# Issuing the stores of the stages between the loops from SyncE instead of ScalarE: a selective-scan and attention kernel on Trainium2

## The chip, the cores and the metric

The kernel runs on one core of a Trainium2 chip. The metric is the device time of one execution in microseconds (us). Engines are named as in the profile: PE (TensorE), DVE (VectorE), ACT (ScalarE), POOL (GpSimd) and SP (SyncE). A transfer between memories (DMA) is started by an instruction in the queue of one engine, here ACT or SP; the profile writes ACTq and SPq for such instructions. Each engine works through its own list of instructions, and they meet through semaphores.

## The reference

Four images of 64 x 64 tokens with 96 channels go through four layers. Layers 0 and 1 are the ones that the change touches: group norm, an input projection to 192 channels with a gate z, a depthwise 3 x 3 convolution, a selective scan in four directions (rows, columns, and both backwards), layer norm, the gate, an output projection and a residual sum. Layers 2 and 3 are linear attention and a feed-forward network on the tokens. The part behind the transfers in question, cut to what matters:

```python
x_dbl = jnp.einsum('bkdl,kcd->bkcl', xs, x_proj_weight)
dts, Bmat, Cmat = jnp.split(x_dbl, [R, R + N], axis=2)
delta = jax.nn.softplus(jnp.einsum('bkrl,kdr->bkdl', dts, dt_projs_weight) + dt_projs_bias[None, :, :, None])
...
def step(h, inp):
    u, d, b, c = inp
    dA = jnp.exp(d[..., None] * A)
    h = dA * h + d[..., None] * b[:, :, None, :] * u[..., None]
    y = jnp.einsum('bken,bkn->bke', h, c)
    return (h, y)
```

For each direction the kernel therefore needs three things before the scan: delta, the product delta times u (called du), and the rows B and C (called bc).

## The kernel before, in words

**Phases.** A pair of images in one of the two scan layers is a phase; there are four. `run` (L701) goes through them: for phase p it runs `prepare` (L151), in which `finish` (L548) of phase p - 1 is mixed by means of Python generators, and then `scan_phase` (L471), the loop. After the fourth loop the last `finish` runs alone, and `token_layers` follows. What the change calls the stages between the loops are `prepare` and `finish`; intermediate results go from them to the loops, and back, through buffers in HBM (`ph.delta`, `ph.du`, `ph.bc`, `ph.ud`, `ph.y`).

**prepare.** It reads the input, makes the group norm statistics, and calls `convolve` (L234) for the first image of the pair. `convolve` loads raw slices (rawi, L244, by SP), normalises them into a padded image xn (L248, DVE), runs nine matmuls for each chunk of 512 positions (L263), and writes Silu of the sum to xc (L270, ACT). It ends with sixteen pieces of xu, xc scaled by the skip weights (L277, ACT), each stored to `ph.ud` (L283). Then for each of the two images, eight chunks and two directions with their backward twins, `steps` (L285) runs: 32 calls, each one step in what follows. The second image's `convolve` is mixed into the first image's steps. The generator's yields and `ph.beside` set how many pieces of the previous phase's `finish` are placed beside each step: 0.5 during the second convolution, 1.7 after it.

**A step.** PE projects the chunk (L292); ACT copies the result to xd in both time directions (L295, L296), and bc is stored from it (L304, two stores, one for each direction). PE makes delta's argument (L309), and then for each of the two directions: ACT softplus to dl (L317) and a bf16 copy to parts[0] (L318); DVE du = dl times u (L319) and the remainder dl - parts[0] (L320); two stores of du to two copies in HBM (L322); POOL parts[1] (L323), DVE parts[2] (L324): delta is kept as three bf16 terms; two stores of delta, one for each half of the channels (L326). The tiles xd, dl, parts and du_sb come from a pool with two buffers, so a buffer is free again when its stores have landed.

**finish.** In four quarters, each in two halves of the channels: SP loads ud_f (L573, four) and yk (L583, eight), PE puts the four directions back in order and adds them up (L596, L605), ACT copies to s (L612). Two slices for each quarter follow (`finish_slice`, L623): xs is loaded (L629, SP), layer norm (L635 to L650, DVE with small ACT operations), the gate (L662 PE, L665 ACT), transposes (L676 PE, L683 ACT), the output projection (L687 PE), the residual sum xo (L689, DVE) and the store of xo (L695). Most tiles of finish have one buffer, yk has four.

**What sets the order.** Inside `scan_phase` the order is written by hand (`manual_schedule`), and all its transfers are issued by SP. In the stages between the loops it is not: the framework's scheduler orders each engine's list when the kernel is built, from its own estimate of durations and from the order of the program, and puts in the semaphores. The list is then fixed, and each engine, ACT and SP alike, takes its instructions in that order. In these stages ACT issues the stores at L283, L304, L326, L695 and one copy of du at L322; SP issues the other copy of du and every load.

Of the kernel before, what the change touches and what calls it, by code (L numbers as in the profile page):

```python
# [23 lines left out]
E = 192  # L24
NS = 16
# [30 lines left out]
def scan_view(t, k, c):  # L56


    part, half = t.ap[0], t.ap[1]
    if k == 0:  # L60
        off, steps = TC * c, (HW, 1)
    elif k == 1:
        off, steps = ROWS * c, (1, HW)
    elif k == 2:
        off, steps = L - 1 - TC * c, (-HW, -1)
    else:
        off, steps = L - 1 - ROWS * c, (-1, -HW)
    return bass.AP(t.tensor, t.offset + off, [part, half, [steps[0], ROWS], [steps[1], HW]])


def view(t, off, *dims):

    return bass.AP(t.tensor, t.offset + off, [t.ap[0]] + [list(d) for d in dims])


def rows(t):

    if len(t.shape) == 2:
        return t.rearrange("p (r w) -> p r w", w=HW)
    return t.rearrange("p h (r w) -> p h r w", w=HW)  # L80
# [50 lines left out]
class Scans:  # L131
# [102 lines left out]
    def convolve(self, ph, i, x, xc, taps, conv_b, dsum):  # L234


        nc = self.nc
        with self.tc.tile_pool(name="conv", bufs=1) as cp:
            xn = cp.tile([C, PAD, PAD], F32, name="xn")
            for edge in (xn[:, 0, :], xn[:, PAD - 1, :], xn[:, 1 : PAD - 1, 0], xn[:, 1 : PAD - 1, PAD - 1]):  # L240
                nc.vector.memset(edge, 0.0)
            for hl in range(8):
                raw = cp.tile([C, 8, 8, 8], F32, name="rawi", bufs=2)
                nc.sync.dma_start(  # L244
                    raw.rearrange("c a h w -> c a (h w)"), x[:, hl * 8 : hl * 8 + 8, i]
                )
                yield
                nc.vector.tensor_scalar(  # L248
                    view(xn, (1 + hl) * PAD + 1, (1, 8), (8 * PAD, 8), (8, 8)),
                    raw,  # L250
                    ph.gs[:, i, 0:1],
                    ph.gs[:, i, 1:2],
                    ALU.subtract,
                    ALU.mult,
                )
            for h in range(2):
                for c in range(NC):
                    if c % 2 == 0:
                        yield
                    ps = self.bank()  # L260
                    for tap in range(9):
                        dy, dx = divmod(tap, 3)
                        nc.tensor.matmul(  # L263
                            rows(ps[:C]),
                            taps[:, tap, h * C : (h + 1) * C],
                            xn[:, ROWS * c + dy : ROWS * (c + 1) + dy, dx : dx + HW],
                            start=tap == 0,
                            stop=tap == 8,
                        )
                    nc.scalar.activation(  # L270
                        xc[:, h, c * TC : (c + 1) * TC], ps[:C], AF.Silu, bias=conv_b[:, h : h + 1]
                    )
            for h in range(2):
                for hl in range(8):
                    yield
                    xu = cp.tile([C, 8, 64], F32, name="xu", bufs=2)
                    nc.scalar.activation(  # L277
                        xu.rearrange("c w (a b) -> c w a b", b=8),
                        view(xc[:, h], hl * HW, (1, 8), (8 * HW, 8), (8, 8)),
                        AF.Copy,  # L280
                        scale=dsum[:, h : h + 1],
                    )
                    nc.scalar.dma_start(ph.ud[:, h, 8 * hl : 8 * hl + 8, i], xu)  # L283

    def steps(self, ph, sp, xc, xp, dt_w, i, k, c):  # L285


        nc, cst = self.nc, self.cst
        u = scan_view(xc, k, c)
        ps = self.bank()  # L290
        for h in range(2):
            nc.tensor.matmul(rows(ps[:XD2]), xp[:, k, h], u[:, h], start=h == 0, stop=h == 1)  # L292
        xd = sp.tile([XD2, TC], F32, name="xd")

        nc.scalar.activation(xd[:XD], ps[:XD], AF.Identity, bias=cst.one_row[:XD])  # L295
        nc.scalar.activation(  # L296
            xd[64:], view(ps[64:XD2], TC - 1, (-1, TC)), AF.Identity, bias=cst.one_row[64:]
        )
        yield
        both = []  # L300
        for back in range(2):
            at = 64 * back
            g, cc = 2 * (k + 2 * back) + i, NC - 1 - c if back else c
            nc.scalar.dma_start(ph.bc[cc][:, g], xd[at : at + 2 * NS])  # L304
            both.append((g, cc, scan_view(xc, k + 2 * back, cc), self.p_d.tile([C, 2, TC], F32, name="d")))
        for m in range(2):
            for back, (_, _, _, ps) in enumerate(both):
                part = slice(64 * back + 2 * NS, 64 * back + XD)
                nc.tensor.matmul(  # L309
                    ps[:, m], dt_w[part, k, m * C : (m + 1) * C], xd[part], start=True, stop=True  # L310
                )
        yield
        for g, cc, u, ps in both:
            delta = sp.tile([C, 2, TC], F32, name="dl")
            parts = sp.tile([C, NP16, 2, TC], BF16, name="parts")
            du = sp.tile([C, 2, TC], F32, name="du_sb")
            nc.scalar.activation(delta, ps, AF.Softplus)  # L317
            nc.scalar.copy(parts[:, 0], delta)  # L318
            nc.vector.tensor_tensor(rows(du), rows(delta), u, ALU.mult)  # L319
            nc.vector.tensor_tensor(delta, delta, parts[:, 0], ALU.subtract)  # L320
            for copy, queue in enumerate((nc.scalar, nc.sync)):
                queue.dma_start(ph.du[cc][copy, g, :E].rearrange("(h e) t -> e h t", h=2), du)  # L322
            nc.gpsimd.tensor_copy(parts[:, 1], delta)  # L323
            nc.vector.tensor_tensor(parts[:, 2], delta, parts[:, 1], ALU.subtract)  # L324
            for h in range(2):
                nc.scalar.dma_start(  # L326
                    ph.delta[cc][:, g, h * C : (h + 1) * C].rearrange("n q t -> q n t"),
                    parts[:, :, h],
                )
            yield  # L330
# [292 lines left out]
    def finish_slice(self, ph, fp, x, x_out, in_w, out_w, gam, bet, hp, wb, s):  # L623

        nc, cst = self.nc, self.cst
        xs = fp.tile([C, 8, 128], F32, name="xs")
        for hi in range(2):
            at = (2 * hp + hi) * 8 + 4 * wb
# [42 lines left out]
        for hi in range(2):  # L671
            yt = fp.tile([C, 2, TC], F32, name="yt")
            for h in range(2):
                ps = self.bank_f()
                for w in range(4):
                    nc.tensor.matmul(  # L676
                        ps[:C, w * 128 : (w + 1) * 128],
                        s[:, 4 * hi + w, h * C : (h + 1) * C],
                        cst.unit,
                        start=True,  # L680
                        stop=True,
                    )
                nc.scalar.copy(yt[:, h], ps[:C])  # L683
                yield
            o = self.bank_f()
            for h in range(2):
                nc.tensor.matmul(o[:C], out_w[:, h], yt[:, h], start=h == 0, stop=h == 1)  # L687
            xo = fp.tile([C, TC], F32, name="xo")
            nc.vector.tensor_tensor(  # L689
                xo, o[:C], xs[:, 4 * hi : 4 * hi + 4].rearrange("c w p -> c (w p)"), ALU.add  # L690
            )
            yield
            yield
            at = (2 * hp + hi) * 8 + 4 * wb
            nc.scalar.dma_start(  # L695
                x_out[:, at : at + 4].rearrange("c a i p -> c (a i p)"), xo
            )

# [292 lines left out]
```

## Time and profile before

| what | value |
|---|---|
| median of 3 runs | 12219.6 us (12207.12 to 12226.98) |
| the profiled execution, its own time | 12191.39 us |
| its span, first to last instruction | 12189.6 us |
| mean granted TensorE clock | 0.856 of full speed |
| PE busy | 9338.7 us (77%) |
| DVE busy | 9363.7 us (77%) |
| ACT busy | 7063.0 us (58%) |
| POOL busy | 7391.0 us (61%) |
| transfers issued by ACT | 512 delta, 256 bc, 256 du, 128 ud, 64 xo |

The busy times leave out the instructions that issue transfers or wait on semaphores: an engine that stands at such an instruction counts as idle, though nothing behind it in its list can start. The span falls into these parts, read from windows of the trace: first prepare up to about 745 us; four loops, 745 to 2620, 3525 to 5400, 6300 to 8180 and 9090 to 10990; between them three mixed stages of about 900 us each, prepare of one phase beside finish of the one before; the last finish, 10990 to 11330; the token layers to the end. In each prepare stage the convolution comes first and the steps after it: in the first stage the part with steps alone begins at about 400, in the mixed ones at about 3040, 5815 and 8597.

The delta stores are 288 KB each, the du stores 384 KB, bc 64 KB, ud and xo 192 KB. Median durations of one issue: delta on ACT 328 ns, bc on ACT 646 ns, ud on ACT 312 ns, xo on ACT 358 ns, du 363 ns on ACT and 305 ns on SP.

### The profile page before, as it was taken

The page shows a single profiled execution, that of the slowest core. Times are in us where ns is not written, and L with a number is a line of the kernel's source. Part 1 is how long each engine was busy: PE and PEld are TensorE (multiplying, and loading weights), DVE is VectorE, ACT ScalarE, POOL GpSimd, SP SyncE. Part 2 cuts the span into 40 slices and gives each one's busy share as a digit, 9 for nine tenths or more (in the row PEclk, how much of TensorE's full clock was granted, in tenths as well). Part 3 has the DMA queues.
Part 4 walks back from the last instruction along what each step waited for, and adds up shares of the span by engine and source line. Part 5 has one row for each costly group of instructions (what it writes and reads, how often), then busy time and mean ns, then how long its engine had stood idle before and what let it go on. Part 6 is the DMA issues. An engine that isn't in the chain of part 4 may idle for free.

```text
span 12189.6 us, 340681 instructions
## 1 busy us (share of the span) xinstructions
PE 9338.7 (77%) x147008; PEld 4884.4 (40%) x147008; DVE 9363.7 (77%) x9235; ACT 7063.0 (58%) x11815; POOL 7391.0 (61%) x2316
## 2 busy tenths in 40 slices
PE   7757777769877777769877777768877777776777
PEld 2224444433334444433334444433334444444333
DVE  2479999963569999982569999982459999993667
ACT  2456666643456666653457666653447666662556
POOL 0159999950149999960139999970119999990000
PEclk8669999989779999989778998988778999998887
DMA  3577777744667777754567777764567777773110
GB/s 95 168 228 257 257 254 254 253 167 142 207 211 256 254 254 255 254 199 130 180 217 257 257 258 255 256 215 125 172 201 251 254 254 254 254 249 124 18 21 11
DMA packets 906195, 2491.48 MB, mean 204 GB/s; under 512 B 278030, under 2 KB 560756, under 8 KB 773236
## 3 DMA queue, kind: packets, MB, share of 16 engines
q1 hardware_dynamic: 578036, 2163.43, 52.2%
q10 hardware_dynamic: 326656, 306.25, 8.5%
q8 instruction: 1158, 18.97, 0.7%
q14 instruction: 345, 2.83, 0.1%
HBM read 1955.47 MB, written 513.80 MB: 203 GB/s over the span
## 4 chain that ended last, share of the span: by engine, by line
DMA 57%; PE 20%; SPq 9%; DVE 5%; ACT 4%; issue 3%; POOL 1%; ACTq 1%; DVEq 0%; POOLq 0%
DMA h<-du 52%; SPq L401 9%; PE c L263 8%; PE f L596 2%; PE d L309 2%; DMA yk<-y 1%; PE c L292 1%; DMA delta<-parts 1%; PE f L605 1%; PE f L687 1%; PE f L676 1%; POOL parts L323 1%; DVE parts L324 1%; PE f L662 1%; PE ph L806 1%
## 5 line engine op out<-in xcount | busy, mean ns | idle before, releaser
L411 POOL TENSOR_TENSOR h<-h,b 128x1536 f32<-128x1536 f32 x2048 | 7021.7, 3462 | 527.6 <-DMA h<-du 187.1
L428 DVE TENSOR_TENSOR_SCAN h<-a,carry,h 128x512 f32<-128x512 f32 x5376 | 6347.5, 1259 | 176.7 <-POOL h L411 174.0
L421 ACT ACTIVATE a<-a,a_col 128x512 f32<-128x512 f32 x6144 | 4035.0, 664 | 1869.5 <-PE a L417 1831.7
L446 PEld LDWEIGHTS y<-h,cw 128*32 128x32 f32 x131072 | 2785.2, 128 | 3513.8 <-issue 1328.8
L446 PE MATMUL y<-h,cw 128*32 128x48 f32 x131072 | 3658.5, 266 | 523.3 <-DVE h L428 217.4
L417 PE MATMUL a<-dlt,rep 72*128 72x512 bf16 x6144 | 2529.7, 422 | 1315.1 <-DVE h L428 1228.6
L323 POOL CAST parts<-dl 96x1024 bf16<-96x1024 f32 x256 | 341.2, 1348 | 3092.4 <-DVE dl L320 2708.9
L319 DVE TENSOR_TENSOR du_sb<-dl,xc 96x1024 f32<-96x1024 f32 x256 | 396.2, 1574 | 1292.5 <-ACT dl L317 1241.5
L458 ACT COPY d<-y 128x384 f32<-128x384 f32 x2048 | 979.8, 478 | 468.2 <-PE y L446 418.4
L263 PE MATMUL c<-xn,taps 96*96 96x512 f32 x2304 | 1033.2, 609 | 73.2 <-DVE xn L248 70.8
L428 DVE TENSOR_TENSOR_SCAN h<-a,h 128x512 f32<-128x512 f32 x768 | 868.1, 1200 | 167.5 <-DMA h<-du 69.3
L417 PEld LDWEIGHTS <-rep 72*128 72x128 bf16 x6144 | 486.4, 98 | 829.4 <-issue 566.5
L309 PE MATMUL d<-xd,dt_w 7*96 7x512 f32 x1024 | 518.2, 856 | 255.7 <-ACT xd L295 224.9
L263 PEld LDWEIGHTS c<-xn,taps 96*96 96x96 f32 x2304 | 382.8, 167 | 707.4 <-issue 629.2
L828 POOL MEMSET tn<- 1x4096 f32 x8 | 27.8, 3506 | 861.8 <-PE pa L848 511.9
L270 ACT ACTIVATE xc<-c,conv_b 96x512 f32<-96x512 f32 x128 | 87.3, 682 | 714.3 <-PE c L263 628.2
L596 PE MATMUL f<-yk,perm 128*128 128x384 f32 x1024 | 417.1, 547 | 94.9 <-DMA yk<-y 90.4
L324 DVE TENSOR_TENSOR parts<-dl,parts 96x1024 bf16<-96x1024 f32 x256 | 366.9, 1455 | 154.3 <-POOL parts L323 154.3
L317 ACT ACTIVATE dl<-d 96x1024 f32<-96x1024 f32 x256 | 251.9, 1017 | 392.5 <-DMA delta<-parts 228.2
L292 PE MATMUL c<-xc,x_proj 96*103 96x512 f32 x512 | 421.8, 961 | 4.2 <-ACT xc L270 4.2
L309 PEld LDWEIGHTS d<-xd,dt_w 7*96 7x96 f32 x1024 | 151.9, 212 | 544.6 <-ACT xd L295 296.8
L363 ACT ACTIVATE cw<-c,gmask 128x256 f32<-128x256 f32 x512 | 285.6, 569 | 118.4 <-DMA c<-bc 62.2
(114 smaller groups left out, 5641.4 us busy)
## 6 DMA issues: line engine op xcount, KB each, us to landing
h<-du SPq DMA_DIRECT2D x1024, 768.0 KB
h<-du SPq DMA_DIRECT2D x2048, 384.0 KB
delta<-parts ACTq DMA_DIRECT2D x512, 288.0 KB
dlt<-delta SPq DMA_DIRECT2D x512, 288.0 KB
du<-du_sb SPq DMA_DIRECT2D x256, 384.0 KB
du<-du_sb ACTq DMA_DIRECT2D x256, 384.0 KB
y<-d SPq DMA_DIRECT2D x2048, 48.0 KB
yk<-y SPq DMA_DIRECT2D x256, 384.0 KB
```

The source lines that it names most:

```text
L263: nc.tensor.matmul(rows(ps[:C]), taps[:, tap, h * C : (h + 1) * C], xn[:, ROWS * c + dy : ROWS * (c + 1) + dy, dx : dx + HW], start=tap == ...
L292: nc.tensor.matmul(rows(ps[:XD2]), xp[:, k, h], u[:, h], start=h == 0, stop=h == 1)
L309: nc.tensor.matmul(ps[:, m], dt_w[part, k, m * C : (m + 1) * C], xd[part], start=True, stop=True)
L324: nc.vector.tensor_tensor(parts[:, 2], delta, parts[:, 1], ALU.subtract)
L401: self.nc.sync.dma_start(u.h[32 * first : 32 * (first + quarters), e : e + n].rearrange("p e t -> p (e t)"), source.rearrange("a g e t -> ...
L411: self.nc.gpsimd.tensor_tensor(h, h, b, ALU.mult)
L417: self.nc.tensor.matmul(u.a[n], self.cst.rep[:, h], u.dl[:, e], start=True, stop=True)
L421: self.nc.scalar.activation(u.a[n], u.a[n], AF.Exp, scale=u.ph.a_col[:, at : at + 1])
L428: self.nc.vector.tensor_tensor_scan(u.h[:, n], u.a.pop(n), u.h[:, n], 0.0 if u.c == 0 else u.ph.carry[:, at : at + 1], ALU.mult, ALU.add,)
L446: self.nc.tensor.matmul(view(u.y[32 * j : 32 * j + 32], l2 * EB, (8 * EB, 4), (1, EB)), u.ph.cw[u.c][:, l1, 8 * j + l2], view(u.h, 64 * l1 ...
L458: self.nc.scalar.copy(u.d[:, :, :, l1], u.y[:, : 32 * EB].rearrange("p (t h x) -> p t h x", t=4, h=2))
L596: nc.tensor.matmul(ps[:, : 4 * C].rearrange("p (w v e) -> p w v e", w=4, v=nv), cst.perm[:, k], view(t, off, (sw if k < 2 else -sw, 4), (1 ...
```

## The change

Each of the five places that issued a store from ACT now issues it from SP. Sources, destinations, sizes and the tiles with their numbers of buffers stay, and so does the order in the program. No transfer of the kernel is issued by ACT afterwards.

```diff
@@ convolve
-                    nc.scalar.dma_start(ph.ud[:, h, 8 * hl : 8 * hl + 8, i], xu)
+                    nc.sync.dma_start(ph.ud[:, h, 8 * hl : 8 * hl + 8, i], xu)
@@ steps
-            nc.scalar.dma_start(ph.bc[cc][:, g], xd[at : at + 2 * NS])
+            nc.sync.dma_start(ph.bc[cc][:, g], xd[at : at + 2 * NS])
...
-            for copy, queue in enumerate((nc.scalar, nc.sync)):
-                queue.dma_start(ph.du[cc][copy, g, :E].rearrange("(h e) t -> e h t", h=2), du)
+            for copy in range(2):
+                nc.sync.dma_start(ph.du[cc][copy, g, :E].rearrange("(h e) t -> e h t", h=2), du)
             nc.gpsimd.tensor_copy(parts[:, 1], delta)
             nc.vector.tensor_tensor(parts[:, 2], delta, parts[:, 1], ALU.subtract)
             for h in range(2):
-                nc.scalar.dma_start(
+                nc.sync.dma_start(
                     ph.delta[cc][:, g, h * C : (h + 1) * C].rearrange("n q t -> q n t"),
                     parts[:, :, h],
                 )
@@ finish_slice
-            nc.scalar.dma_start(
+            nc.sync.dma_start(
                 x_out[:, at : at + 4].rearrange("c a i p -> c (a i p)"), xo
             )
```

## The prediction

> **What bounds it.** I read the busy windows first, cut at the borders of the stages, because the page's shares average over stages with different limits. Columns: length, then busy us of PE, PEld, DVE, ACT, POOL (instructions in brackets), granted TensorE clock, share of the 16 DMA engines, GB/s.
>
> ```profile
> 400.00:745.00 345.00, 189.04 (x280) 58.44 (x278) 195.94 (x138) 133.06 (x148) 66.65 (x46) 0.51 0.67 198
> 745.00:2620.00 1875.00, 1431.59 (x34004) 810.61 (x34008) 1797.50 (x1532) 1283.94 (x2284) 1754.12 (x512) 0.91 0.73 253
> 2620.00:3040.00 420.00, 346.14 (x1132) 139.47 (x1121) 126.39 (x173) 134.45 (x160) 25.68 (x19) 0.87 0.40 118
> ...
> 5815.00:6300.00 485.00, 392.37 (x1120) 195.18 (x1118) 277.23 (x358) 227.70 (x290) 61.67 (x48) 0.72 0.64 198
> ```
>
> The loops (second line; four of them, some 7,500 us) are held by DVE, 1797 of 1875 us, and POOL; no edited transfer is in them. A stage between loops has two parts. In the convolution part (third line) PE is busy 346 of 420 us. In the step part no engine is near full: 196 of 345 us at most in the first stage, and 392 of 485 on a PE at clock 0.72 in a mixed stage (steps beside the last phase's finish). So something that isn't counted as busy binds there. The timeline of ACT in the first stage shows it (start, length, engine, line, operation, count, idle before and its releaser):
>
> ```profile
> 586.06 1.93 ACT L317 ACTIVATE dl<-d 96x1024 f32<-96x1024 f32 x2 [8.17 <-DMA delta<-parts]
> 588.01 1.05 ACT L318 CAST parts<-dl 96x1024 bf16<-96x1024 f32 x1
> 589.08 0.36 ACTq L322 DMA_DIRECT2D du<-du_sb  x1
> 589.56 1.05 ACT L318 CAST parts<-dl 96x1024 bf16<-96x1024 f32 x1 [0.50 <-ACT parts L318]
> 590.90 0.36 ACTq L322 DMA_DIRECT2D du<-du_sb  x1
> 591.31 0.68 ACT L295 ACTIVATE xd<-c,one_row 39x512 f32<-39x512 f32 x1 [0.71 <-DVE du_sb L319]
> 592.02 0.68 ACT L296 ACTIVATE xd<-c,one_row 39x512 f32<-39x512 f32 x1
> 596.18 2.65 ACTq L326 DMA_DIRECT2D delta<-parts  x4
> 598.93 1.79 ACTq L304 DMA_DIRECT2D bc<-xd  x2
> 600.77 1.93 ACT L317 ACTIVATE dl<-d 96x1024 f32<-96x1024 f32 x2 [8.07 <-DMA delta<-parts]
> ```
>
> One step is all ten lines. ACT is done with the step's arithmetic at 592.70, then stands at the delta stores until DVE has written parts (3.5 us), issues six transfers (4.5 us), and only then starts the next step's dl at 600.77. Yet PE's L309 matmuls for that dl began at 592.05 and took 4.43 us: their results lay ready at 596.48. ACT's place in its own queue costs 4.3 us of a 14.3 us step (from 557.97 to 600.77 are three steps).
>
> Added up over ACT's instructions in the trace (issue time, and the gap ahead of an issue): in 400 to 745 it issues 192 transfers for 102 us and stands 97 us ahead of them; with 133 us of work only 7 us of its time are left over. In 5815 to 6300 it is 211 transfers, 77 us and 108 us, beside 228 us of work and 73 us of other waits. PE's waits in that mixed window (us, times, longest):
>
> ```profile
> PE d L309 <- ACT xd L295: 21.7, 4, 7.8
> PE f L687 <- ACT yt L683: 19.0, 4, 7.3
> PE f L662 <- ACT z L665: 17.6, 5, 6.7
> PE f L596 <- DMA yk<-y: 9.7, 5, 4.1
> PE d L309 <- ACT xd L296: 7.9, 3, 4.7
> ```
>
> The four ACT lines make 66.2 us; the landing of yk only 9.7.
>
> **The skill.** "TensorE: Matmul & The Clock Gate", section "Architectural detail", says that ACT's queue is strict FIFO: the trace agrees, the dl above sits behind stores that it doesn't need. "DMA: Bandwidth & Descriptors", section "Issuing engines are not separate DMA queues", says that transfers of all issuers share the same 16 engines and that a second issuer saves only issue time. The trace agrees on the first half; on the second it shows that the wait ahead of the issue (97 us) counts as much as the issue (102 us). The same TensorE page, section "Part 1: The HAM clock gate", says that the PE clock falls to half when PE is idle and comes back under load: 0.51 in the first line of the windows, 0.91 in the loop.
>
> **The change, part by part.** All five edits move an issue from ACT to SP; bytes, descriptors and tiles stay.
>
> Delta (four a step, 512), du's first copy (two a step, 256) and bc (two a step, 256), the first stage. Off ACT goes 4.3 us a step, as above, plus about 1.2 us where the du issues hold back parts and xd. A step is then bounded by what comes next: ACT 133/23 = 5.8 us of work (46 du issues in the window, two a step, are 23 steps), DVE 196/23 = 8.5, PE 189/23 = 8.2 at half clock, the DMA engines 0.67 x 345/23 = 10.0 us. DMA is the latest. Is one ring enough for that? While ACT's four delta stores were the only ones moving, it was:
>
> ```profile
> 598.00:600.00 2.00, 2.00 (x3) 0.30 (x1) 0.00 (x0) 0.00 (x0) 0.00 (x0) 0.50 1.00 291
> ```
>
> I allow a DMA share of 0.9[...]: 10.0/0.9 = 11.2 us a step, 3.1 less than 14.3. Over 23 steps: **71 us**. Bounds: 18 us if the slots of parts (two buffers, freed by the landing of the delta stores) hold the step at 13.5 us; 94 us if the DMA share reaches 0.92 of the whole window (231/0.92 = 251 against 345).
>
> The same edits in the three mixed stages. ACT is not busy for 485 - 228 = 257 us, and 186 of them, 0.72, are at transfers (77.3 + 108.4). I take that share of PE's 66.2 us of waits for ACT as gone: 48 us a stage, **144 us** for three. What is late next is DVE (277 of 485), the landing of yk, and the shares of DMA (0.64). Bounds: 0 if these take over at once; 97 a stage if DMA, 0.64 x 485 = 310 us, is driven at 0.8 and PE regains clock; below nothing is the rival below.
>
> What SP takes on. In 5815 to 6300 SP issues 123 transfers in 69 us; 211 with 77 us are added, 146 of 485 us. Issue prices are alike: du 305 ns on SP, 363 on ACT. But SP too works in order. A delta store that waits for DVE L324 now stands ahead of the du and bc stores of the next step, and of the finish's loads ud_f L573, yk L583, xs L629 and the convolution's rawi L244; PE L596 and L605, DVE L654 and L248 wait for those. The other way, stores stand behind blocks of loads. du shows how often: its two copies wait for the same DVE instruction, and SP's left more than 10 us after ACT's for 2 of 47 in the window, over 2 us for 4. I cost it at nothing beyond the 28 percent of PE's waits that I left standing.
>
> ud (L283, 128 stores) belongs to the convolution part: PE is what ends ACT's waits there. Nothing; bounds -5 to 10 us in all. The xo stores (L695, 64): those beside steps are in the 144. In the last finish (10990 to 11330) ACT loses 5 us of issue and 35 of standing, but has 211 us of other idle time; SP's xs loads there wait for the same DVE L689 as the stores. Nothing; bounds -10 to 10. No such transfer is in the loops or the token layers.
>
> Sum: 71 + 144 = 215 us. The profiled execution took 12191.4 us (span 12189.6), which gives 11,976; the median of the runs shown is 28 us above it, 12219.6, which gives **12,005 us**. Its own band, first stage 40 to 94 and mixed 25 to 75 each, is 11,900 to 12,105.
>
> **Rivals.**
> Slower: SP becomes what ACT was. A half quarter of the finish loads four ud_f and eight yk in one block, 13 to 14 us of SP (from 6095.06 to 6108.43). If a store behind a block is on the path, and the two slots of parts and du_sb don't bridge it, each of 8 blocks in 3 stages costs 14 us, 336 in all, against the 215: 12,341. It decides once 215/336, 64 percent of the blocks, are exposed. For it: two of the lags above are 13.5 and 13.9 us, just such blocks. Against: only those two of 47. 0.17.
> No change: landings rather than issues hold the step. The slots keep it at 13.5 us (18 us gained) and the mixed stages gain nothing as DVE and yk take over: 12,202. For it: chain pieces of delta<-parts of 3.5 us in nearly every step; against: these contain ACT's own issue. 0.12.
> Much faster: the DMA limits are reached everywhere, 94 + 3 x 97 = 385: 11,835. For it: the clock, at 0.51 and 0.72, has room; against: two streams that feed each other seldom pack so well. 0.15.
> That the change doesn't do what it says is excluded: the five issues are explicit. But outside the loops the scheduler orders the queues anew from its own estimate, which widens all cases.
>
> **Numbers.** My forecast has 0.56. The range, 11,850 to 12,260, leaves out half of the fast rival (0.08) and most of the slow one (0.12). The measurement can tell 0.2 percent, 24 us, from no change: faster 0.56 + 0.15 = 0.71, same 0.12, slower 0.17.
>
> **What would show it.** In the changed profile: no ACTq transfers; the first stage's step near 11.2 us and its part some 71 us shorter, DMA share near 0.85; ACT's dl L317 released by PE or DVE; the mixed parts near 437 us with a clock over 0.72; loops within 0.2 percent. I am wrong if SP's waits on DVE L324 come before late yk landings in PE's waits, or if ACT's L318 waits for landings of delta.

## The result: 0.87 percent faster, half of the forecast

| | median (runs) | ratio to before, 95% interval | profiled execution |
|---|---|---|---|
| before | 12213.36 us (12198.66 to 12226.98, 4) | 1 | 12191.39 |
| changed | 12109.49 us (12096.0 to 12114.05, 4) | 0.9913 [0.9896, 0.9931] | 12114.05 |

The direction was forecast, and the time lies in the range, but 215 us were forecast and the ratio gives 106 (0.0087 x 12213). To see where the rest went I cut both traces at the scans (L428): a stage is the time from the last scan of a loop to the first of the next, the first stage runs from the start. A step is here, as in all that follows, the mean distance of two steps' L317 between 450 and 700 us.

| us | first stage | mixed stages | four loops together | step of the first stage |
|---|---|---|---|---|
| before | 774.0 | 927.3, 929.5, 939.1 | 7416 | 14.3 |
| forecast | -71 | -48 each | within 0.2% | 11.2 |
| changed | 753.1 (-20.9) | 905.3, 908.8, 903.7 (-22.0, -20.7, -35.4) | 7433 | 13.0 |

The stages gave 99 us. The loops differ by 0.2 percent, which single loops also do between executions (1837 to 1870 us in all versions below). So what is missing is missing where the gain was expected: 50 us in the first stage, 66 in the three others. First the windows of the changed kernel, the step parts of the first stage and of two mixed stages, and a stretch of the second that is used again below (columns as in the prediction):

```profile
412.00:738.00 326.00, 237.33 (x284) 62.44 (x283) 182.40 (x138) 132.86 (x148) 75.50 (x46) 0.52 0.75 222
3040.00:3490.00 450.00, 384.81 (x1085) 190.34 (x1084) 265.03 (x351) 218.37 (x280) 72.72 (x46) 0.74 0.68 210
5785.00:6262.00 477.00, 396.74 (x1102) 198.02 (x1101) 267.23 (x353) 219.04 (x282) 72.52 (x46) 0.71 0.66 206
5790.00:6225.00 435.00, 373.98 (x1031) 184.09 (x1029) 256.13 (x344) 209.29 (x269) 70.25 (x44) 0.72 0.67 207
```

The DMA share of the first stage rose from 0.67 to 0.75 where 0.85 was forecast: transfers are not what binds. The timeline of the first stage, all engines, of which I show one chain (start, length, engine, line, operation, tiles, count, idle before and its releaser):

```profile
592.60 1.02 ACT L317 ACTIVATE dl<-d 96x1024 f32<-96x1024 f32 x1 [2.47 <-DVE parts L324]
...
595.86 1.22 DVE L319 TENSOR_TENSOR du_sb<-dl,xc 96x1024 f32<-96x1024 f32 x1
...
599.32 1.02 ACT L317 ACTIVATE dl<-d 96x1024 f32<-96x1024 f32 x1 [4.64 <-DVE parts L324]
...
600.24 1.03 ACT L318 CAST parts<-dl 96x1024 bf16<-96x1024 f32 x1
...
601.30 1.22 DVE L320 TENSOR_TENSOR dl<-dl,parts 96x1024 f32<-96x1024 f32 x1 [2.08 <-ACT parts L318]
...
602.65 1.04 POOL L323 CAST parts<-dl 96x1024 bf16<-96x1024 f32 x1 [4.68 <-DVE dl L320]
...
603.72 1.22 DVE L324 TENSOR_TENSOR parts<-dl,parts 96x1024 bf16<-96x1024 f32 x1 [1.19 <-POOL parts L323]
...
605.03 1.02 ACT L317 ACTIVATE dl<-d 96x1024 f32<-96x1024 f32 x1 [2.47 <-DVE parts L324]
...
612.45 1.02 ACT L317 ACTIVATE dl<-d 96x1024 f32<-96x1024 f32 x1 [5.33 <-DVE parts L324]
```

ACT no longer stands at stores, but its L317 now waits for DVE's L324, the last reader of a dl buffer; there are two. And the cast at 600.24 belongs not to the dl written at 599.32 but to the one of 592.60: the du of that older tile, which must precede its L320, is the DVE line at 595.86, and the L320 at 601.30 waits for this cast. The older dl was ready at 593.6. Its cast came 6.6 us later, because in ACT's list it stands behind the next tile's L317, and that one waited 4.64 us for a buffer. Each dl thus passes L317, the next L317, cast, L320, L323 and L324 before it is free: 5.7 and 7.4 us for the two tiles, 13.1 for the step (599.32 to 612.45). In the changed kernel's list 177 of 256 casts stand like this, in the list of the kernel before 100. The edit does not name these instructions; the scheduler orders the lists anew.

In a mixed stage PE waits so (PE's waits, 5790 to 6225: us, times, longest):

```profile
PE f L596 <- DMA yk<-y: 16.0, 7, 4.7
PE f L662 <- DVE xm L654: 13.8, 4, 5.1
PE d L309 <- ACT xd L295: 13.0, 3, 9.0
PE f L676 <- DVE s L669: 8.4, 3, 4.7
...
PE f L662 <- ACT z L665: 1.1, 1, 1.1
```

ACT's part of PE's waits fell from 66.2 to about 15 us, a little more than forecast. But yk is later (9.7 before), and of DVE's lines xm is longer (4.6 before; s was 7.0). SP now stands where ACT stood, as its own waits in the same stretch show:

```profile
SPq L326 <- DVE parts L324: 107.1, 30, 11.4
SPq L695 <- DVE xo L689: 41.8, 9, 9.6
```

What stands behind such a wait, from SP's timeline:

```profile
6100.20 0.32 SPq L695 DMA_DIRECT2D x<-xo  x1
6100.56 0.43 SPq L322 DMA_DIRECT2D du<-du_sb  x1
...
6108.77 0.31 SPq L695 DMA_DIRECT2D x<-xo  x1
6109.13 0.91 SPq L629 DMA_DIRECT2D xs<-in_x  x2
6110.08 0.43 SPq L322 DMA_DIRECT2D du<-du_sb  x1
```

And from DVE's timeline, when the data of these stores were written:

```profile
6091.31 3.75 DVE L319 TENSOR_TENSOR du_sb<-dl,xc 96x1024 f32<-96x1024 f32 x2
...
6099.48 0.69 DVE L689 TENSOR_TENSOR xo<-f,xs 96x512 f32<-96x512 f32 x1
...
6108.05 0.69 DVE L689 TENSOR_TENSOR xo<-f,xs 96x512 f32<-96x512 f32 x1 [2.94 <-PE f L687]
```

DVE finished the second du at 6095.06. Its two copies left at 6100.56 and 6110.08, each behind an xo store whose data DVE had only just written. Over the window, from the end of a du on DVE to the issue of its later copy (worked out from the trace, the n-th du with its two stores) the mean is 7.2 us; before it was 1.4. In some 3 of the 7.2 us SP stands ahead of other transfers (1.2 us at xo, 0.8 at delta), in most of the rest it issues them (1.1 us for yk). SP issues 318 transfers in 202 us of the 435; before it was 121 in 67 of 460.

So two new waits were candidates: ACT's order with two dl buffers, and SP's order. Each is taken away by itself below, as far as the scheduler leaves the rest as it was. All ratios are to the kernel before, in the same session.

### The profile page after: what moved, and what is told of

Same layout as the page of the kernel before. It is cut to its first block, busy times and chain, and to the rows that moved or that the text cites. A ratio compares the mean times of both kernels' runs of the same rounds, so it can differ in the third digit from the quotient of the medians.

```text
span 12112.3 us, 340525 instructions
## 1 busy us (share of the span) xinstructions
PE 9447.6 (78%) x147008; PEld 4901.4 (40%) x147008; DVE 9331.6 (77%) x9235; ACT 7064.4 (58%) x11818; POOL 7444.5 (61%) x2316
## 4 chain that ended last, share of the span: by engine, by line
DMA 55%; PE 22%; SPq 9%; DVE 6%; ACT 4%; issue 2%; POOL 1%; POOLq 0%; ACTq 0%; DVEq 0%
DMA h<-du 51%; PE c L263 9%; SPq L401 9%; PE f L596 2%; PE d L309 2%; PE c L292 2%; POOL parts L323 1%; PE f L676 1%; DMA yk<-y 1%; DVE parts L324 1%; DVE dl L320 1%; PE f L687 1%; PE f L605 1%; PE f L662 1%; ACT parts L318 1%
## 5 line engine op out<-in xcount | busy, mean ns | idle before, releaser
L428 DVE TENSOR_TENSOR_SCAN h<-a,carry,h 128x512 f32<-128x512 f32 x5376 | 6350.0, 1259 | 189.2 <-POOL h L411 186.3
L323 POOL CAST parts<-dl 96x1024 bf16<-96x1024 f32 x256 | 395.7, 1549 | 2910.9 <-DVE dl L320 1884.2
L428 DVE TENSOR_TENSOR_SCAN h<-a,h 128x512 f32<-128x512 f32 x768 | 869.6, 1201 | 160.6 <-ACT a L421 131.6
L309 PE MATMUL d<-xd,dt_w 7*96 7x512 f32 x1024 | 610.2, 845 | 112.3 <-ACT xd L295 80.0
L320 DVE TENSOR_TENSOR dl<-dl,parts 96x1024 f32<-96x1024 f32 x256 | 310.2, 1217 | 326.1 <-ACT parts L318 324.6
L317 ACT ACTIVATE dl<-d 96x1024 f32<-96x1024 f32 x256 | 258.6, 1019 | 398.6 <-DVE parts L324 373.9
L596 PE MATMUL f<-yk,perm 128*128 128x384 f32 x1024 | 414.1, 546 | 81.5 <-DMA yk<-y 81.1
L324 DVE TENSOR_TENSOR parts<-dl,parts 96x1024 bf16<-96x1024 f32 x256 | 324.3, 1272 | 192.2 <-POOL parts L323 182.8
L292 PE MATMUL c<-xc,x_proj 96*103 96x512 f32 x512 | 425.0, 968 | 2.9 <-ACT xc L270 2.3
L309 PEld LDWEIGHTS d<-xd,dt_w 7*96 7x96 f32 x1024 | 164.0, 209 | 502.2 <-issue 206.5
```

The lines of the kernel that those rows point to most:

```text
L309: nc.tensor.matmul(ps[:, m], dt_w[part, k, m * C : (m + 1) * C], xd[part], start=True, stop=True)
L428: self.nc.vector.tensor_tensor_scan(u.h[:, n], u.a.pop(n), u.h[:, n], 0.0 if u.c == 0 else u.ph.carry[:, at : at + 1], ALU.mult, ALU.add,)
L596: nc.tensor.matmul(ps[:, : 4 * C].rearrange("p (w v e) -> p w v e", w=4, v=nv), cst.perm[:, k], view(t, off, (sw if k < 2 else -sw, 4), (1 ...
```

## Experiments

### The buffers of dl and du_sb

To make room for a third buffer, rawi and xu, in the convolution, get one buffer each instead of two. `room` is the changed kernel with that alone.

```diff
-                raw = cp.tile([C, 8, 8, 8], F32, name="rawi", bufs=2)
+                raw = cp.tile([C, 8, 8, 8], F32, name="rawi")
-                    xu = cp.tile([C, 8, 64], F32, name="xu", bufs=2)
+                    xu = cp.tile([C, 8, 64], F32, name="xu")
```

> The changed kernel with one buffer less for rawi and for xu, which only makes room for the next two kernels. Every theory: within 15 us of the changed kernel's 12109 us, the step of the first stage at its 12.9 us; it is the measure for the next two.

Measured: 0.9958 [0.9942, 0.9975]; stages 759.3, then 927.5, 920.0, 921.4. Making room costs 33 us by the medians, 55 by the ratios (0.0045 x 12200), more than the 15 expected; the changed kernel was timed in another session.

```diff
# room_dl3, on room
-            delta = sp.tile([C, 2, TC], F32, name="dl")
+            delta = sp.tile([C, 2, TC], F32, name="dl", bufs=3)
```

> As the kernel with room, and a third buffer for dl. Theory (after the change the two buffers of dl hold the step: one is held from L317 to the end of L324, and each is used once a step): ACT's waits for DVE L324 go, the step falls from 12.9 to about 11.3 us, where PE's 11.2 us a step at half clock are next; 23 steps give some 35 us in the first stage, 5 to 15 us in each mixed stage, 50 to 80 us in all against the kernel with room. Rival (landing of du or delta holds the step): the wait moves to L318 or L319, step 12.5 us or more, under 15 us in all. Rival (the DMA engines bound it): no gain, DMA share as before.

Measured: 0.9855 [0.9836, 0.9874], 129 us less than room (medians 12142.61 and 12013.15). But the step fell only from 13.2 to 12.7 us, not to 11.3; the gain came in the mixed stages, 35 us each. The buffer matters, though the theory put its gain in the wrong place. In this kernel's list even more casts, 221 of 256, stand behind the next tile's L317.

```diff
# room_du3, on room
-            du = sp.tile([C, 2, TC], F32, name="du_sb")
+            du = sp.tile([C, 2, TC], F32, name="du_sb", bufs=3)
```

> As the kernel with room, and a third buffer for du_sb instead. Theory (dl's buffers hold the step): the product L319 can follow dl at once, which shortens the time that dl is held by a part of the 4.5 us it waits now, so the step falls by at most 1 us, 10 to 30 us in all. Rival (landing of the du stores holds the step): the step falls to 11.3 us, 50 to 80 us in all. Third view (DVE's order is what counts, not the buffers): the same as the rival, with dl still waiting for L324.

Measured: 0.9916 [0.9899, 0.9934], 51 us less than room, mixed stages 907.8, 906.8, 911.6: 10 to 20 us each, more than expected. The two slots of du_sb, free only when their stores have landed, cost something too.

The same room and third dl buffer in the kernel before:

> The kernel before, transfers on ScalarE as they were, with one buffer for rawi and xu and three for dl, the two edits that made the changed kernel 129 us faster (relative to room) and cost it 33 us (room). Theory (the two dl buffers became the bound only because ScalarE's queue no longer was): the step of the first stage stays within 13.8 to 14.3 us, the mixed stages gain nothing, and the ratio to before is 1.000 to 1.005, as making room costs up to 33 us. Rival (a third dl buffer is worth its 129 us whichever engine issues): 0.992 to 0.995.

Measured: 1.0106 [1.0091, 1.0121], step 14.4 us, mixed stages 960.9, 972.2, 981.4. The rival falls: with the stores on ACT the two edits together lose 1.1 percent, where the rival had them gain. Making room costs more here than expected: the stretch from a loop's end to the end of the convolution's matmuls grew from 422 to 450 us. No run has the room alone in the kernel before, so what the third buffer does by itself there is not shown.

### Parts of the change

Only the delta stores on SP, the four other edits left out:

```diff
# on the kernel before
-                nc.scalar.dma_start(
+                nc.sync.dma_start(
                     ph.delta[cc][:, g, h * C : (h + 1) * C].rearrange("n q t -> q n t"),
```

> The kernel before with the four delta stores a step (L326) on SyncE and nothing else moved; du's first copy, bc, ud and xo stay on ScalarE. Theory (ScalarE lost its time by standing in order ahead of stores whose data come late; only the delta stores have late data, 3.5 us of standing and 2.65 us of issue a step of 7.6): this part alone gives at least two thirds of the full change, ratio to before 0.991 to 0.995. Rival (ScalarE's issue time as such was what cost, spread over all five edits; the delta stores are half of the transfers): about half, 0.995 to 0.997. Second rival (SyncE's own order costs in the full change: with du, bc and xo kept off it, this beats the full change): 0.986 to 0.990.

Measured: 0.9791 [0.9773, 0.9809], 11971.20 us; step 11.5; stages 711.0, 872.4, 887.3, 876.5. One of five edits gains 2.1 percent, more than twice the whole change, and more than even the second rival asked for. The other four together cost 1.2 percent. So I put them back singly.

xo (L695) back on ACT:

> The changed kernel with the 64 xo stores back on ACT. Theory (in the mixed stages SP's order costs: yk loads stand behind xo stores that wait for DVE, and so do the loop's first loads): the 11 us between the last delta store and the first load of the loop shrink to under 6 us in each of three stages, yk comes earlier, 15 to 50 us faster in all than the changed kernel. Rival (SP's order costs nothing there, the mixed stages are held by PE and by the finish's own chain): within 10 us, and ACT gets some 35 us of standing back in the last finish without effect.

Measured: 0.9898 [0.9877, 0.9919]; mixed stages 900.4, 890.0, 908.3. The interval overlaps the changed kernel's; at most a small part.

bc (L304) back on ACT:

> The changed kernel with the bc stores (L304, 256 transfers, two a step as du's first copy) back on ScalarE. 132 of 256 L318 stand behind the next L317. Theory A: about half of what the order costs comes back, less than with du's first copy, 0.983 to 0.988. Rival B: as with du's first copy, by number, 0.985 to 0.987, or more than it, as a bc issue takes SyncE about twice as long.

Measured: 0.9881 [0.9867, 0.9894], step 13.1, mixed stages 901.8, 882.1, 899.4. Less than both theories asked for.

du's first copy (L322) back on ACT:

> The changed kernel with du's first copy (L322, 256 transfers) back on ScalarE. Its L318 stand behind the next tile's L317 in 106 of 256 cases, almost as where only delta is moved (86; changed kernel 177). Theory A (ScalarE's order is what the other edits cost): most of the lost 1.3 percent comes back, ratio 0.979 to 0.984, step under 12.2. Rival B (what SyncE has to issue is what costs): a share by number, du is 256 of the 640 transfers that make the difference to moving delta alone, 40 percent, 0.985 to 0.987.

Measured: 0.9813 [0.9796, 0.9831], step 11.8, stages 723.2, 879.7, 868.1, 872.5. It gives back 1.0 of the 1.2 percent, far more than its share by number and than bc, which is as many transfers. But it does more than one thing: ACT's list changes back (106 casts behind the next L317), du leaves earlier (mean lag 4.1 us), and the scheduler orders the lists of PE and DVE anew too.

### ACT's order alone

All stores stay on SP; each L317 is put behind the cast of the tile before it in ACT's list (an order, no wait):

```diff
... (self.last is None at the start)
-            nc.scalar.activation(delta, ps, AF.Softplus)
-            nc.scalar.copy(parts[:, 0], delta)
+            soft = nc.scalar.activation(delta, ps, AF.Softplus)
+            if self.last is not None:
+                self.tc.add_manual_dep(
+                    soft.ins, self.last.name,
+                    mybir.DependencyInfo(mybir.DependencyClass.NoSync, mybir.DependencyReason.DATA),
+                    reason="order",
+                )
+            self.last = nc.scalar.copy(parts[:, 0], delta).ins
```

> The changed kernel, every transfer on SyncE, with one thing set: on ScalarE each L317 (writes dl) stands behind the L318 (casts dl) of the tile before it. In the changed kernel 177 of the 256 L318 stand behind the next tile's L317, which waits for a free dl; in the kernel with only delta moved 86 of 256. Theory A (this order is what the other four edits cost: two dl buffers, each held through the next L317, give 2 x 6.5 us a step): step of the first stage 11 to 12 us instead of 13.0, first stage 30 to 45 us shorter, mixed stages 20 to 45 each, ratio 0.979 to 0.985. Rival B (SyncE is overcharged: du and bc stores stand behind delta stores and loads, and one ring carries all): no gain, 0.989 to 0.993. Between them, both count.

Measured: 0.9868 [0.9854, 0.9881], 12061.32 us. It splits the question. The first stage fell from 753.1 to 702.5 us, its step to 10.9: theory A. The mixed stages stayed at 901.5, 906.7, 906.0: rival B. The window 420 to 660 of the changed kernel:

```profile
420.00:660.00 240.00, 195.97 (x228) 51.65 (x226) 146.10 (x111) 105.55 (x118) 59.05 (x37) 0.51 0.76 222
```

The same window of `pin`:

```profile
420.00:660.00 240.00, 218.81 (x252) 59.32 (x250) 180.82 (x132) 119.94 (x132) 52.27 (x45) 0.50 0.88 265
```

The DMA share is 0.88. ACT's timeline in it, and the longest of its waits (lines behind the edit are 6 higher here: the cast is L324, L324 is L330):

```profile
593.88 1.05 ACT L324 CAST parts<-dl 96x1024 bf16<-96x1024 f32 x1 [2.12 <-DMA delta<-parts]
594.95 1.02 ACT L317 ACTIVATE dl<-d 96x1024 f32<-96x1024 f32 x1
...
600.49 1.02 ACT L317 ACTIVATE dl<-d 96x1024 f32<-96x1024 f32 x1 [1.29 <-DVE parts L330]
...
ACT parts L324 <- DMA delta<-parts: 100.2, 42, 6.6
```

What ends ACT's waits is now the landing of delta, with every store on one issuer. That the transfers alone bind, as forecast, is not shown by this run: PE is busy too, 218.81 of 240 us, and from 550 to 610 even 59.64 of 60. In the kernel with delta alone moved the DMA share is 0.88 as well, with PE busy only 180.06 of the same 240 us and a step of 11.5; that speaks for the transfers. A third buffer of parts, which would tell the transfers' rate from their slots, was not tried.

### TensorE's order

In the changed kernel the eight L309 matmul records of a step, one row group after the other, come as four and four, 3.72 us each; before they ran as eight in 4.43 us. `pair` keeps the written order of these matmuls among themselves, in which the two row groups (one for each direction) alternate:

```diff
-        for m in range(2):
-            for back, (_, _, _, ps) in enumerate(both):
...
+        with self.tc.manual_schedule(engines={mybir.EngineType.PE}):
+            for m in range(2):
+                for back, (_, _, _, ps) in enumerate(both):
...
```

> The changed kernel with the four L309 matmul instructions of a step kept in the order they are written in on TensorE (both row groups alternate, so that they can run side by side), nothing else. Theory A (the two dl buffers hold the step; TensorE's split order is only a consequence of the second dl's wait): no gain, first stage step 12.9 to 13.3, ratio 0.990 to 0.993, as the changed kernel. Theory B (the split costs TensorE about 3 us of a step at half clock and this is what the mixed stages, where TensorE is busiest, lack): mixed stages 15 to 35 us shorter each, ratio 0.983 to 0.987. It may also be slower, if holding the first pair for the second buffer of d delays the first dl: up to 0.996.

Measured: 0.9886 [0.9871, 0.9900], step 13.0, stages 752.0, 895.9, 895.3, 899.8: 4 to 13 us in a mixed stage and nothing in the first. The eight records now come as two and six, 2.02 and 3.72 us, with matmuls of L292 in between, so the split is made smaller and not undone. That its cost falls from 7.4 to 5.7 us without any change of the step shows that it does not hold the first stage of the changed kernel.

### Combinations

`best` is room_dl3 with xo on ACT:

> The changed kernel with one buffer for rawi and xu, three for dl, and the xo stores back on ScalarE: the two variations that gained something, together. Theory (the third dl buffer shortens the step, the xo stores on ScalarE let a phase's finish end with its steps; two places, so the gains add): 10 to 30 us below the third buffer alone, ratio 0.983 to 0.985. Rival (the finish is hidden behind the steps and loses to ScalarE's order what it gains on SyncE): as the third buffer alone, 0.984 to 0.987.

Measured: 0.9840 [0.9827, 0.9854], mixed stages 884.0, 888.8, 877.4; room_dl3 had 891.8, 885.2, 885.3. No gain over it that can be told.

`pin_du` is `pin` with du's first copy on ACT:

```diff
# on pin
-            for copy in range(2):
-                nc.sync.dma_start(ph.du[cc][copy, g, :E].rearrange("(h e) t -> e h t", h=2), du)
+            for copy, queue in enumerate((nc.scalar, nc.sync)):
+                queue.dma_start(ph.du[cc][copy, g, :E].rearrange("(h e) t -> e h t", h=2), du)
```

> The changed kernel with both: ScalarE's order set (each L317 behind the L318 of the tile before) and du's first copy (L322) back on ScalarE. Theory (two separate causes: ScalarE's order holds the first stage, setting it took that from 753 to 703 us and left the mixed stages at 901 to 907; du's copies late on SyncE hold the mixed stages, taking one copy off took these from 906 to 868 to 880 and the first stage only to 723): the gains add, first stage 700 to 715, mixed stages 865 to 885, ratio 0.977 to 0.981. Rival 1 (one cause, ScalarE's order, seen twice): mixed stages about 900, ratio 0.985 to 0.988. Rival 2 (du's issue on ScalarE, waiting for VectorE's L319, brings the old standing back): first stage 723 or more, ratio 0.980 to 0.983.

Measured: 0.9751 [0.9737, 0.9765], 11895.02 us, the fastest of all; step 10.9; stages 704.0, 864.9, 861.5, 864.1. The gains add, and somewhat more. The later copy of du leaves 2.6 us after DVE's end in the mean. PE's waits in the mixed window 5690 to 6080 (L602 is L596 here, L682 is L676):

```profile
PE d L309 <- ACT xd L295: 13.5, 3, 5.7
PE f L682 <- DVE s L675: 8.3, 3, 4.5
...
PE f L602 <- DMA yk<-y: 1.2, 2, 0.8
```

That window:

```profile
5690.00:6080.00 390.00, 357.23 (x1054) 174.26 (x1052) 254.08 (x342) 220.03 (x278) 58.29 (x44) 0.79 0.77 235
```

PE's waits for yk and xm are all but gone, the DMA share is 0.77 instead of 0.67, and PE was granted a clock of 0.79 instead of 0.72.

## Why the prediction was half right

**What bounds the kernel now: right.** ACT's place in its own queue, behind delta stores that wait for DVE, was the bound. Moving those stores alone shortens the kernel by 2.1 percent, 255 us, and its stages by 63, 55, 42 and 63.

**The first stage, "A step is then bounded by what comes next ... DMA is the latest", 11.2 us and 71 us: failed as put, by a term that the sum did not have.** I compared busy times and DMA share only. Late next was none of these but two buffers of dl together with a new order of ACT's list: step 13.0, 20.9 us. With that order set the step is 10.9 at a DMA share of 0.88, and the stage 702.5, 71.5 us below 774.0. So the number of the sum came true once the slot was out of the way. Its reason is less sure: I had PE at 8.2 us a step, and in `pin` PE is as full as the DMA engines. My lower bound had the right kind of cause, "18 us if the slots of parts ... hold the step at 13.5 us", but the slots were those of dl.

**The mixed stages, 48 us each: the wait went, the gain did not follow.** PE's waits for ACT fell from 66 to about 15 us, and the stages by 22, 21 and 35. With delta alone moved the waits fell as far as I had put it, to 22 us (5715 to 6130), and the stages by 55, 42 and 63: this term was sound as long as SP took on little else. The step that failed is "What SP takes on. ... I cost it at nothing beyond the 28 percent". The four other edits cost the mixed stages 33, 21 and 27 us. Two terms under it were wrong. Issue: I put SP at 69 + 77 = 146 us of 485; it is 202 of 435. The 77 us are only what ACT's issues took beside its arithmetic, and their whole length was 107; the rest is that one issue takes longer there, 0.64 us in the mean, against 0.53 for the same kinds of transfers on two queues; the 305 ns that I had for du were of issues that stand apart. Place: I read du's lag from a queue that held only half of the stores (2 of 47 late by 10 us); with xo, bc and delta in it the mean lag is 7.2 us. My slower rival had the idea, "SP becomes what ACT was", but blocks of loads are the smaller part of that lag, and it gave the cost all or nothing.

Taking only du's first copy off SP shortens the mixed stages by 26, 41 and 31 us; ACT's order alone changes them by 4 at most; both together make them 62, 68 and 75 shorter than before, more than the 48 forecast.

**What SP's waits would show.** I named late yk as a sign of failure, and it came, 9.7 to 16.0 us. I also named ACT's L318 waiting for landings of delta: a badly chosen sign, for it is what the full gain looks like in `pin` (100 us in 240). L317 is released by DVE, as I wrote, but I had taken that as a mark of success, when it was the new bound.

**ud and xo, nothing:** xo back on ACT changes less than can be told; ud was not tried by itself. The last finish is 342.3 us before and 343.2 after.

**The scheduler.** That it "orders the queues anew ... which widens all cases" was right, but it decided about 50 us of the first stage and could not be read from the profile of before.

**Smaller slips.** Of ACT's 345 us in the first stage 13 are left over, not 7 (345 - 102 - 97 - 133). And in the two microseconds that I read as delta stores alone, 598 to 600, the first bc store was already issued (598.93).

**What stays open.** Moving du's first copy back to ACT gains 37 to 45 us a mixed stage with ACT's order set in both kernels (`pin`, `pin_du`). That du's lateness is the path is only argued, and three things speak against it as the whole cause. The lists change with the edit: in the second mixed stage only 370 of DVE's 522 instructions keep their order among themselves from `pin` to `pin_du`. In room_dl3 du is as late as in the changed kernel (mean lag 7.3 us), yet its mixed stages are 885 to 892 us. And DVE's wait for du's landing, 25.6 us in the window of the changed kernel, is 8.9 with the copy on ACT but 19.7 in `pin_du`, whose stages are shorter. SP's loads leave earlier as well. Why a third dl buffer helps the mixed stages by 35 us, where setting ACT's order does not, wasn't settled either. bc, whose issue takes SP longest, cost little alone. The single parts give back 1.0 (du), 0.3 (bc) and 0.15 percent (xo), 1.5 together where 1.2 are missing, which agrees within the intervals of the runs.

## What to carry to other kernels

In this kernel it paid to move the store whose data come late, and to leave those alone whose data are ready when their own engine gets to them. A store fits on a queue whose other waits end no later than its own data. When a wait is taken off a path, look not only at which engine or transfer is busiest next but at every buffer on the path: who reads it last, how many there are, and how long one is held. And where lists are ordered by a scheduler, an edit to a few transfers can reorder arithmetic that it doesn't touch; compare the lists before the mechanism is judged. That holds for the experiments too: each of the variants here came with orders of its own.

## What the runs showed of the hardware

An issue has no fixed price; it goes with what the same queue issued just before. du on SP in a mixed window took 304/307/1517 ns before (min, median, max). After, in the answer for the tile du_sb:

```profile
L322 SPq DMA_DIRECT2D du<-du_sb x92: 304/449/1539, 5797.5 to 6232.2; - x92
```

Of these 92, the 75 that followed another issue of SP within 0.2 us took 600 ns in the mean, the 17 others 386. Before, 43 of 47 stood apart, 336 ns in the mean.

A merged line of the timeline can hide a wait: four delta stores in the kernel with delta alone moved show as one line of 6.70 us (593.05), but they are two pairs of 0.8 us each, and between them SP waits 5.1 us for DVE's second tile.

"DMA: Bandwidth & Descriptors" of the Trainium skill, section "Issuing engines are not separate DMA queues", has it that a second issuer saves only issue time. Here du's copy on ACT took 17 us of issue off SP (202 in 435 us, then 185 in 385), and the stage became 41 us shorter. The waits in SP's queue went down with it (at delta stores from 107 to 90 us, at xo stores from 42 to 16) and the lists were ordered anew, so the run doesn't refute the sentence, but issue time alone doesn't account for the gain.

One issuer kept the transfers going at 265 GB/s, share 0.88, over 240 us with every store on SP.

The same eight matmul records of L309 took 4.43 us when the two row groups alternated and 7.4 when one followed the other, with a clock of 0.5 in both.

A busy PE did not get its clock back: in the first stage of `pin` PE was busy 59.64 of 60 us (550 to 610) at a clock of 0.50, while the mixed window of `pin_du`, busy 357.23 of 390 us, had 0.79. "TensorE: Matmul & The Clock Gate" of the Trainium skill, section "Part 1: The HAM clock gate", which the prediction cites, has the clock come back under load; by these figures the busy share alone does not decide it.
